# Second attention of a two-layer block model: the kernel gives the order of instructions on four engines

## The chip, the cores and the metric

The kernel runs on one core of a Trainium2 chip. The metric is the device time of one execution in microseconds, as the median of several runs. PE is the matrix engine, with PEld its weight loads; DVE, ACT and POOL are the vector, scalar and GpSimd engines; SP issues transfers.

## The reference

The input is 16 sequences of 256 tokens with 256 features in float32. Two layers follow each other, and every sub-layer is added to its input and normalized:

```
x = layernorm(x + L0_attn(x))   # receptance, key, value; a decaying scan over time
x = layernorm(x + L0_ffn(x))    # gated feed-forward, weights dequantized
x = layernorm(x + L1_attn(x))   # latent attention: 16 heads, two-sequence batches, causal softmax
x = layernorm(x + L1_ffn(x))    # 32 experts, 4 chosen per token, and a shared expert
```

The change is in the third line. There, for one sequence and one head:

```
cq     = rms_norm(x @ w_qa.T);  q = cq @ w_qb.T          # 128 plain and 64 rotated columns a head
ckv    = x @ w_kva.T;  k_pe = rotated(ckv[64:]);  c = rms_norm(ckv[:64])
scores = (q_nope . k_nope + q_pe . k_pe) * scale, masked above the diagonal
out    = softmax(scores) @ v;   x = layernorm(x + concat(out) @ w_o.T)
```

The fourth line needs a routing decision for each token (sigmoid scores, the best 3 of 8 groups, the best 4 experts in them) and a slot for each token and expert.

## The kernel before

The 4096 tokens are cut into 8 blocks of 512 tokens, which is two sequences each. The stages run one after the other: first attention, feed-forward, second attention, the rest of the shared expert, the experts, and the sum. The code is written for a tile framework whose scheduler decides the order of instructions on each engine from the dependencies and from its own costs; `tc.issue_after(x)` keeps a few instructions behind another one. Each engine then works through its own queue in that order.

In the second attention a step is a pair of heads of a block, so there are 64 steps. Keys and queries of a head are folded into the latent space beforehand (`w_q`, `w_qr`), and values with the output weights (`w_ov`).

- `latents(b)` (L742) is done once a block: eight PE transposes of the input, four latent products with squares on ACT, two inverse roots (`rsqrt`: DVE, then a power on POOL), scaling on DVE into `cq` and `kf`, rotation of the key part (`kr`), and twelve PE transposes, with copies by DVE (`cqT`) and ACT (`kT`).
- `queries` (L820) makes `q_ps` for both heads in two PSUM tiles of the tag `m`; `turn` (L837) rotates each with three DVE products from PSUM and one POOL addition.
- `attend` (L851) is one head in one sequence. PE writes scores in two parts, 128x128 and 128x256, which leave out the masked quarter. DVE adds the mask and takes the extreme (L868), ACT takes the exponential with its row sum (L878), DVE takes the reciprocals (L886, L887), POOL divides (L888).
- `keys_first` (L896) transposes the result on PE, ACT copies it. `contexts` (L906) multiplies it by the latents of the keys, two heads beside each other in the array.
- `stage_contexts` (L926) copies the contexts into `cT` on DVE (L935), and after four pairs multiplies by `w_ov`, which adds half an output to `x` (L945); after eight pairs `added` adds the other half and normalizes.
- `choose` (L554) and `place` (L636) route the block before: some sixty small DVE instructions and a few matmuls. `scatter` (L669) writes one token tile for one choice with an indirect transfer by POOL. `shared_glu` and `shared_down` (L688, L702) are the shared expert, done here for three blocks.

The PSUM has eight banks: three for the tag `m` (queries, latents, outputs, router and shared expert take turns in them), two for scores, two for transposes, one for contexts.

The loop over steps (L966) writes the queries of step i, the softmax of step i-1 and the contexts of step i-2, and the latents of the next block at its sixth step. The routing of a block is written into the first and third steps of the next block, its scatters into the softmax of steps 4 to 7. The scheduler moves all of this within the dependencies.

Of the kernel before, what the change touches and what calls it, by code (L numbers as in the profile page):

```python
# [86 lines left out]
def seq_postln_kernel(ctx: ExitStack, tc: tile.TileContext, a: dict, out: bass.AP, cap: int):  # L87
# [42 lines left out]
    def layernorm(ys, dsts):  # L130
        n = len(ys)
        mv = small.tile([P, n, 2], F32, tag=f"mv{n}", name="mv")
        for i, y in enumerate(ys):
            st = small.tile([P, 6], F32, tag="bn", name="bn")
            nc.vector.bn_stats(st, y)
            nc.vector.bn_aggr(mv[:, i, :], st)
        rstd = small.tile([P, n], F32, tag=f"rstd{n}", name="rstd")
        rsqrt(rstd, mv[:, :, 1], 1.0, LN_EPS)
        for i, (y, dst) in enumerate(zip(ys, dsts)):
            nc.vector.tensor_scalar(  # L140
                dst, y, mv[:, i, 0:1], rstd[:, i : i + 1], ALU.subtract, ALU.mult
            )

# [403 lines left out]

    SH_EARLY = 3
# [5 lines left out]
    def choose(b, psum, tag):  # L554

        xT = xTs[b] = transposed(b, mo_x, psum, tag)
        l_ps = psum.tile([P, BLK], F32, tag=tag, name="l_ps")[:, : GT * E].rearrange(
# [11 lines left out]

        last_of["PE"] = mm.ins  # L570

        sco = tl("sco", GT, E)
        nc.scalar.activation(sco, l_ps, AF.Sigmoid)
        sc = tl("sc", GT, E)
# [12 lines left out]
        tt_(gs.rearrange("p n g -> p (n g)"), m1, m2, ALU.add)  # L587

# [17 lines left out]
        )  # L606

# [3 lines left out]
        for k in range(K):  # L611
# [5 lines left out]
            if k < K - 1:  # L617
                nc.vector.scalar_tensor_tensor(
                    left, chosen[:, k], TAKEN, left, ALU.mult, ALU.add
                )  # L620
        big, wt = tl("big", K, GT, E), tl("wt", K, GT)
# [6 lines left out]
        tt_(wt, wt, top.unsqueeze(1).to_broadcast([P, K, GT]), ALU.mult)  # L628

# [4 lines left out]
        return sel, chosen, big, eq  # L634

    def place(b, psum, tag, chose):  # L636

        sel, chosen, big, eq = chose
# [87 lines left out]
    with ExitStack() as ph:  # L726
        pl = ph.enter_context(tc.tile_pool(name="lat", bufs=2))
        pq = ph.enter_context(tc.tile_pool(name="q2", bufs=3))
# [11 lines left out]
        X2 = X1 + HR  # L740

        def latents(b):  # L742


            xT = transposed(b, mo_x, ps_m, "m")
            lat = pl.tile([P, NTT, QLR + KVLR + DR], F32, tag="lat", name="lat", bufs=1)
            ss = pl.tile([P, 2, NTT], F32, tag="ss", name="ss")
            sq = pl.tile([P, QLR], F32, tag="sq", name="sq")
            for tt in range(NTT):
# [9 lines left out]
                nc.scalar.copy(lat[:, tt, :], ps)  # L759
                for k, (lo, n) in enumerate(((0, QLR), (QLR, KVLR))):  # L760
# [6 lines left out]
            rms = pl.tile([P, 2, NTT], F32, tag="rms", name="rms")  # L767
            rsqrt(rms[:, 0, :], ss[:, 0, :], 1.0 / QLR, RMS_EPS)
            rsqrt(rms[:, 1, :], ss[:, 1, :], 1.0 / KVLR, RMS_EPS)
            cq = pl.tile([P, NTT, 2 * P], F32, tag="cq", name="cq", bufs=1)  # L770
            kf = pl.tile([P, NTT, P], F32, tag="kf", name="kf")
            for tt in range(NTT):
# [9 lines left out]
                )  # L782
                nc.vector.scalar_tensor_tensor(
# [7 lines left out]
            kr = pl.tile([P, NTT, DR], F32, tag="kr", name="kr")  # L791
# [4 lines left out]

            cqT = pl.tile([P, 2, BLK], F32, tag="cqT", name="cqT")
            for j in range(2):
                ps = ps_m.tile([P, BLK], F32, tag="m", name="cqT_ps")
                for tt in range(NTT):  # L800
# [3 lines left out]
                nc.vector.tensor_scalar(  # L804
                    cqT[:, j, :], ps, q_ln[:, j : j + 1], None, ALU.mult
                )
            kT = pl.tile([P, BLK], F32, tag="kT", name="kT")
# [4 lines left out]
            return cqT, kf, kT  # L812
# [7 lines left out]
        def queries(cqT, pair):  # L820

            pss = []
            for k in range(2):
                ps = ps_m.tile([P, BLK], F32, tag="m", name="q_ps")
                mm = nc.tensor.matmul(  # L825
# [3 lines left out]
            with tc.issue_after(mm.ins):  # L829
                for k, ps in enumerate(pss):  # L830
                    rows = slice(k * QR, (k + 1) * QR)
                    nc.tensor.matmul(
                        ps, lhsT=w_qr[rows, pair, :], rhs=cqT[rows, 1, :], start=False, stop=True
                    )
            return [turn(ps, 2 * pair + k) for k, ps in enumerate(pss)]

        def turn(ps, h):  # L837
            qT = pq.tile([P, BLK], F32, tag="qT", name="qT", bufs=5)
# [10 lines left out]
        pool_last = [None]  # L849

        def attend(qT, kT, s):  # L851

            ps = ps_s.tile([P, 3 * P], F32, tag="s", name="s_ps")
            sm = pa.tile([P, 3 * P], F32, tag="sm", name="sm")
            pr = pa.tile([P, 3 * P], F32, tag="pr", name="pr", bufs=8)
            nm = pa.tile([P, 2], F32, tag="nm", name="nm")
            rs = pa.tile([P, 2], F32, tag="rs", name="rs")
            rr = pa.tile([P, 3], F32, tag="rr", name="rr")
            for i, (lo, hi) in enumerate(parts):
                nc.tensor.matmul(  # L860
                    ps[:, lo:hi],
                    lhsT=qT[:, s * S + i * P : s * S + (i + 1) * P],
                    rhs=kT[:, s * S : s * S + hi - lo],
                    start=True,
                    stop=True,
                )
            for i, (lo, hi) in enumerate(parts):
                nc.vector.tensor_tensor_reduce(  # L868
                    out=sm[:, lo:hi],
                    in0=ps[:, lo:hi],  # L870
                    in1=cst["mask"][:, lo:hi],
                    scale=-(DQ**-0.5),
                    scalar=-MASKED,
                    op0=ALU.add,
                    op1=ALU.min,
                    accum_out=nm[:, i : i + 1],
                )
                nc.scalar.activation(  # L878
                    pr[:, lo:hi],
                    sm[:, lo:hi],  # L880
                    AF.Exp,
                    bias=nm[:, i : i + 1],
                    scale=-1.0,
                    accum_out=rs[:, i : i + 1],
                )
            nc.vector.reciprocal(rr[:, :2], rs)  # L886
            nc.vector.reciprocal(rr[:, 2:], rs[:, 1:])  # L887
            pool_last[0] = nc.gpsimd.tensor_tensor(  # L888
                pr.rearrange("p (i k) -> p i k", k=P),
                pr.rearrange("p (i k) -> p i k", k=P),  # L890
                rr.unsqueeze(2).to_broadcast([P, 3, P]),
                ALU.mult,
            ).ins
            return pr

        def keys_first(pr):  # L896

            a_ps = ps_a.tile([P, 3 * P], F32, tag="a", name="a_ps")
            for i in range(3):
                nc.tensor.transpose(  # L900
                    a_ps[:, i * P : (i + 1) * P], pr[:, i * P : (i + 1) * P], ident
                )
            aT = pa.tile([P, 3 * P], F32, tag="aT", name="aT")
            return aT, nc.scalar.copy(aT, a_ps)  # L904

        def contexts(c_ps, prs, kf, s):  # L906


            aTs, copies = zip(*[keys_first(pr) for pr in prs])
            for i in range(2):  # L910
                for k, aT in enumerate(aTs):
                    mm = nc.tensor.matmul(
                        c_ps[k * KVLR : (k + 1) * KVLR, i * P :],
# [5 lines left out]
                    if i == k == 0:  # L919
                        after(mm.ins, copies[1].ins, "beside the other head's")  # L920
            last_of["ctx"] = mm.ins

        NP = NH // 2
        blocks = {}

        def stage_contexts(b, p, prs):  # L926
            kf = blocks[b][1]
            half_p = p % (NP // 2)
            if half_p == 0:
                cTs[0] = pc.tile([P, NP // 2, BLK], F32, tag="cT", name="cT")  # L930
            cT = cTs[0]
            c_ps = ps_c.tile([P, 2, S], F32, tag="c", name="c_ps")
            for s in range(2):
                contexts(c_ps[:, s, :], prs[2 * s : 2 * s + 2], kf, s)
            nc.vector.tensor_copy(cT[:, half_p, :], c_ps.rearrange("p s t -> p (s t)"))  # L935
            if half_p == NP // 2 - 1:
                os = []
                for s in range(2):
                    ps = ps_m.tile([P, BLK], F32, tag="m", name="o_ps").rearrange(
                        "p (k d) -> p k d", k=2  # L940
                    )
                    for k in range(2):
                        at = (2 * s + k) * P
                        for j in range(NP // 2):
                            nc.tensor.matmul(  # L945
                                ps[:, k, :],
                                lhsT=cT[:, j, at : at + P],
                                rhs=w_ov[:, p - half_p + j, :],
                                start=(j == 0),
                                stop=(j == NP // 2 - 1),  # L950
                            )
                        os.append(ps[:, k, :])
                    if p < NP - 1:
                        x2 = xs[b][:, 2 * s : 2 * s + 2, :D]
                        nc.vector.tensor_tensor(x2, ps, x2, ALU.add)
                if p == NP - 1:
# [3 lines left out]
        def begin(b):  # L960
            blocks[b] = latents(b)
# [272 lines left out]
```

## Time and profile before

| | |
|---|---|
| time, median of 3 runs (lowest to highest) | 2430.03 us (2429.53 to 2431.76) |
| the profiled execution, and its span from first to last instruction | 2428.3 us, 2426.5 us |
| mean granted PE clock | 0.964 |
| PE, DVE, ACT, POOL busy, share of the span | 91%, 55%, 29%, 34% |
| second attention: first transposes of its first block to its last output matmul | 1213.5 to 2170.1 us |
| eight context products of block 5, first start to that of block 6 | 1834.4 to 1951.3 us |

A row of the timeline reads: start, time until the last one ends, engine, line, operation, output <- inputs, shapes and how often in a row. A float32 matmul of the code stands as two records, a transpose as one; matmuls overlap, so the distance between starts says what one costs, and the duration is longer. A row of groups reads: line, engine, operation, shapes and count, then busy time and mean nanoseconds of one, then the idle time of the engine just before and what ended it. In rows of stretches, each engine's busy time has its number of instructions behind it, and the last three columns are the granted PE clock, the share of the transfer engines and GB/s.

### The profile page before, as it was taken

What the parts mean: (1) busy time and instruction counts of PE and PEld (TensorE: products, weight loads), DVE (VectorE), ACT (ScalarE), POOL (GpSimd) and SP (SyncE); (2) the same over time, 40 slices, a digit from 0 to 9 for tenths busy, and PEclk for the clock granted to TensorE, in tenths of its full rate; (3) what the DMA queues carried; (4) which work ended last, traced back from release to release, by engine and by line L of the source; (5) the groups of instructions that cost most, each with busy time, mean ns of one, the idle gap of its engine ahead of it and who ended that gap; (6) DMA issues with size and microseconds to landing.
All of it is one profiled execution on the core that took longest, in us unless ns stands there. A gap on an engine that the chain in (4) does not pass through costs nothing. (4 is left out here: it accounts for less than half of the span.)

```text
span 2426.5 us, 27654 instructions
## 1 busy us (share of the span) xinstructions
PE 2203.7 (91%) x8832; PEld 1325.7 (55%) x8832; DVE 1332.7 (55%) x4052; ACT 708.9 (29%) x2013; POOL 826.9 (34%) x932
## 2 busy tenths in 40 slices
PE   8499999999999999999989888999898888888937
PEld 4255555555555555455556555555555555555826
DVE  4163545454454433222376868686878887855513
ACT  3021212222121112111145445353535344331202
POOL 3021212122211210000054464645555647452671
PEclk9699999999999999999999999999999999999968
DMA  9620000000000003000000000000000000042746
GB/s 301 196 59 0 9 1 9 1 9 1 0 1 1 0 1 111 0 1 0 1 1 1 5 30 2 14 2 13 1 3 2 3 2 3 1 148 86 147 64 263
DMA packets 75793, 90.53 MB, mean 37 GB/s; under 512 B 13719, under 2 KB 66011, under 8 KB 75520
## 3 DMA queue, kind: packets, MB, share of 16 engines
q1 hardware_dynamic: 46208, 59.46, 7.3%
q10 hardware_dynamic: 17152, 21.44, 2.9%
q0 software_dynamic: 12288, 7.87, 2.3%
q8 instruction: 70, 1.15, 0.2%
q14 instruction: 75, 0.61, 0.1%
HBM read 58.29 MB, written 45.21 MB: 43 GB/s over the span
## 5 line engine op out<-in xcount | busy, mean ns | idle before, releaser
L342 POOL TENSOR_TENSOR wkv<-su,r_sb 128x512 f32<-128x512 f32 x128 | 165.3, 1292 | 719.8 <-DVE su L333 685.8
L319 DVE TENSOR_TENSOR kv<-k_sb,proj 128x512 f32<-128x512 f32 x128 | 88.0, 687 | 450.6 <-PE proj L298 406.5
L878 ACT ACTIVATE pr<-sm,nm 128x128 f32<-128x128 f32 (+1 forms) x512 | 228.0, 447 | 251.5 <-DVE nm L868 249.8
L298 PE MATMUL proj<-xm,w_Wr 128*128 128x512 f32 x512 | 242.7, 597 | 35.4 <-ACT k_sb L315 35.4
L888 POOL TENSOR_TENSOR pr<-pr,rr 128x384 f32<-128x384 f32 x256 | 210.6, 829 | 125.5 <-DVE rr L887 76.6
L298 PE MATMUL proj<-xm,w_Wk 128*128 128x512 f32 x512 | 242.5, 596 | 6.8 <-DVE xm L284 6.8
L347 PE MATMUL o_ps<-w_o,wkv 128*128 128x256 f32 x1024 | 245.2, 379 | 0.3 <-POOL st L322 0.2
L347 PEld LDWEIGHTS o_ps<-w_o,wkv 128*128 128x128 f32 x1024 | 194.4, 190 | 89.6 <-issue 67.8
L844 POOL TENSOR_TENSOR qT<-qT,turned 128x512 f32<-128x512 f32 x128 | 166.7, 1306 | 222.1 <-DVE turned L843 214.9
L298 PE MATMUL proj<-xm,w_Wv 128*128 128x512 f32 x512 | 241.4, 594 | 0.0
L315 ACT COPY k_sb<-proj 128x512 f32<-128x512 f32 x128 | 74.9, 585 | 559.5 <-PE proj L298 505.3
L860 PE MATMUL s_ps<-kT,qT 128*128 128x128 f32 (+1 forms) x1024 | 220.9, 352 | 8.7 <-DVE nm L868 6.2
L860 PEld LDWEIGHTS s_ps<-kT,qT 128*128 128x128 f32 x1024 | 152.5, 203 | 61.6 <-DVE nm L868 23.5
L298 PEld LDWEIGHTS proj<-xm,w_Wr 128*128 128x128 f32 x512 | 97.9, 192 | 156.0 <-issue 118.2
L868 DVE CUSTOM_DVE_ANT_0 sm<-s_ps,const 128x128 f32<-128x128 f32 (+1 forms) x512 | 159.6, 352 | 37.5 <-PE s_ps L860 32.3
L324 DVE TENSOR_TENSOR_SCAN st<-decay,kv 128x255 f32<-128x255 f32 x256 | 162.6, 677 | 3.8
L674 POOL DMA_INDIRECT xp_d<-xs,dest x128 | 128.5, 1004 | 100.8 <-DVE dest L659 74.2
L298 PEld LDWEIGHTS proj<-xm,w_Wv 128*128 128x128 f32 x512 | 97.7, 191 | 117.3 <-issue 116.5
L900 PE MATMUL a_ps<-const,pr 128*128 128x128 f32 x768 | 131.3, 286 | 32.4 <-POOL pr L888 30.1
L904 ACT COPY aT<-a_ps 128x384 f32<-128x384 f32 x256 | 117.4, 471 | 142.8 <-PE a_ps L900 139.2
L128 POOL TENSOR_TENSOR rstd<-rs_t,nhalf 128x4 f32<-128x4 f32 x32 | 32.5, 1017 | 350.8 <-DVE rs_t L127 345.9
L825 PE MATMUL q_ps<-cqT,w_q 128*128 128x512 f32 x256 | 135.8, 631 | 8.5 <-DVE turned L843 8.5
(166 smaller groups left out, 3363.0 us busy)
## 6 DMA issues: line engine op xcount, KB each, us to landing
w_e<-in_W_experts_dram SPq DMA_DIRECT2D x32, 384.0 KB
sum<-zeros ACTq DMA_DIRECT2D x2, 4224.0 KB
part<-sum SPq DMA_DIRECT2D x16, 512.0 KB
xp_d<-empty ACTq DMA_DIRECT2D x1, 5300.0 KB
xe<-xp_d SPq DMA_DIRECT2D x32, 165.6 KB
xb<-in_xT_dram SPq DMA_DIRECT2D x16, 256.0 KB
xs<-in_x_dram SPq DMA_DIRECT2D x32, 128.0 KB
sum<-acc SPq DMA_DIRECT2D x16, 256.0 KB
```

What stands on the lines that cost most here:

```text
L298: nc.tensor.matmul(ps, lhsT=w3[name][:, c, h * P : (h + 1) * P], rhs=xm[:, c, :], start=(c == 0), stop=(c == DC - 1),)
L324: nc.vector.tensor_tensor_scan(st[:, s, 1:], decay[:, h : h + 1].to_broadcast([P, S - 1]), kv[:, s, : S - 1], 0.0, ALU.mult, ALU.add,)
L342: nc.gpsimd.tensor_tensor(wkv, su, r_sb, ALU.mult)
L347: nc.tensor.matmul(os[tt], lhsT=wkv[:, tt * P : (tt + 1) * P], rhs=w_o[:, h, :], start=(h == 0), stop=(h == NH - 1),)
L674: put = nc.gpsimd.indirect_dma_start(out=xp_d[:, :], out_offset=bass.IndirectOffsetOnAxis(ap=dest[:, k, t : t + 1], axis=0), in_=xs[b][:, ...
L825: mm = nc.tensor.matmul(ps, lhsT=w_q[:, 2 * pair + k, :], rhs=cqT[:, 0, :], start=True, stop=False)
L844: nc.gpsimd.tensor_tensor(qT, qT, qr, ALU.add)
L860: nc.tensor.matmul(ps[:, lo:hi], lhsT=qT[:, s * S + i * P : s * S + (i + 1) * P], rhs=kT[:, s * S : s * S + hi - lo], start=True, stop=True,)
L868: nc.vector.tensor_tensor_reduce(out=sm[:, lo:hi], in0=ps[:, lo:hi], in1=cst["mask"][:, lo:hi], scale=-(DQ**-0.5), scalar=-MASKED, op0=ALU ...
L878: nc.scalar.activation(pr[:, lo:hi], sm[:, lo:hi], AF.Exp, bias=nm[:, i : i + 1], scale=-1.0, accum_out=rs[:, i : i + 1],)
L888: pool_last[0] = nc.gpsimd.tensor_tensor(pr.rearrange("p (i k) -> p i k", k=P), pr.rearrange("p (i k) -> p i k", k=P), rr.unsqueeze(2).to_ ...
L900: nc.tensor.transpose(a_ps[:, i * P : (i + 1) * P], pr[:, i * P : (i + 1) * P], ident)
```

## The change

The whole second attention now stands under `tc.manual_schedule` for PE, DVE, ACT and POOL: on these engines its instructions run in the order in which the code writes them. Step n of the new loop writes the scores and softmax of pair n+1, the queries of pair n+2 and the contexts of pair n-1, interleaved by hand. `latents` and `choose` with `place` (now `route`) are generators, of eight and nine parts. Their parts, the halves of the output (`output`, now by sequence), the two halves of the norm (`moments`, `normalize`) and the parts of the shared expert are put at two places in each step, by the pair's number p in its block.

Some work changes its form. A softmax now covers both sequences of a head: one reciprocal of 128x4 takes the place of four, and POOL divides in one instruction of 128x2x128 and one of 128x2x256 in place of two of 128x384. The copies of `cT` and the scalings of `cqT` go from DVE to ACT. The buffers of `qT` become six, `pr` becomes six tiles of two sequences, and `sq`, `kr` have one or are taken anew. The scatters of a block come two blocks later, two or three in each step but the first, so those of block 6 now follow the attention.

The diff, cut; `parts`, `scores` and `exps` of the new class `Softmax` hold what `attend` held:

```
-    def choose(b, psum, tag):
+    def route(b, psum, tag):
...
         xT = xTs[b] = transposed(b, mo_x, psum, tag)
+        yield
...
-                nc.vector.tensor_scalar(
-                    cqT[:, j, :], ps, q_ln[:, j : j + 1], None, ALU.mult
-                )
+                nc.scalar.activation(cqT[:, j, :], ps, AF.Copy, scale=q_ln[:, j : j + 1])
...
+            def divide(self):
+                rr = pa.tile([P, 2, 2], F32, tag="rr", name="rr")
+                nc.vector.reciprocal(rr, self.rs)
+                for i, (lo, hi) in enumerate(parts):
+                    nc.gpsimd.tensor_tensor(
+                        self.pr[:, :, lo:hi],
+                        self.pr[:, :, lo:hi],
+                        rr[:, :, i : i + 1].to_broadcast([P, 2, hi - lo]),
+                        ALU.mult,
+                    )
...
-            nc.vector.reciprocal(rr[:, :2], rs)
-            nc.vector.reciprocal(rr[:, 2:], rs[:, 1:])
-            pool_last[0] = nc.gpsimd.tensor_tensor(
-                pr.rearrange("p (i k) -> p i k", k=P),
-                pr.rearrange("p (i k) -> p i k", k=P),
-                rr.unsqueeze(2).to_broadcast([P, 3, P]),
-                ALU.mult,
-            ).ins
...
-            nc.vector.tensor_copy(cT[:, half_p, :], c_ps.rearrange("p s t -> p (s t)"))
...
+        def output(b, half, s):
+            cT = cTs[b, half]
+            ps = ps_m.tile([P, BLK], F32, tag="m", name="o_ps").rearrange("p (k d) -> p k d", k=2)
+            for k in range(2):
+                at = (2 * s + k) * P
+                for j in range(NP // 2):
+                    nc.tensor.matmul(
+                        ps[:, k, :],
+                        lhsT=cT[:, j, at : at + P],
+                        rhs=w_ov[:, half * NP // 2 + j, :],
+                        start=(j == 0),
+                        stop=(j == NP // 2 - 1),
+                    )
+            x2 = xs[b][:, 2 * s : 2 * s + 2, :D]
+            nc.vector.tensor_tensor(x2, ps, x2, ALU.add)
...
+        def first_place(b, p):
+            last = b - 1
+            if p == 3 and last >= 0:
+                x = x_t[last * NTT : (last + 1) * NTT]
+                normalize(x, x, *norms.pop(last))
+            if p == 4:
+                step_latents(b + 1)
+            if p >= 5:
+                step_route(last)
+        def second_place(b, p):
+            last = b - 1
+            if p == 0:
+                step_route(last - 1)
+            if p <= 5 or p == 7:
+                step_latents(b + 2 if p == 7 else b + 1)
+            if p in (1, 2) and last >= 0:
+                output(last, 1, p - 1)
+                if p == 2:
+                    norms[last] = moments(x_t[last * NTT : (last + 1) * NTT])
+            if 3 <= p:
+                step_route(last)
+            if p in (5, 6):
+                output(b, 0, p - 5)
+            if p == 7:
+                shared(last, 0)
+            if p == 0:
+                shared(last - 1, 1)
+            if p == 4:
+                shared(last - 1, 2)
+                shared(last - 1, 3)
+        def scatters(b, p):
+            if b >= 0 and p:
+                lo = 3 * (p - 1) if p < 3 else 6 + 2 * (p - 3)
+                return [(b, j) for j in range(lo, lo + (3 if p < 3 else 2))]
+            return []
+        NS = NB * NP
+        engines = {nc.tensor.engine, nc.vector.engine, nc.scalar.engine, nc.gpsimd.engine}
+        with tc.manual_schedule(engines=engines):
+            qTs, sms = {}, {}
+            for _ in range(8):
+                step_latents(0)
+            step_latents(1)
+            for n in range(-2, NS + 1):
+                b, p = divmod(n, NP)
+                todo = scatters(b - 2, p)
+                def one_scatter():
+                    if todo:
+                        scatter(todo[0][0], [todo.pop(0)[1]])
+                scored = n + 1 if 0 <= n + 1 < NS else None
+                asked = n + 2 if 0 <= n + 2 < NS else None
+                seen = n - 1 if 0 <= n - 1 < NS else None
+                if scored is not None:
+                    kT = latent[scored // NP][2]
+                    heads = sms[scored] = []
+                    qT2 = qTs.pop(scored)
+                    heads.append(Softmax())
+                    for s in range(2):
+                        heads[0].scores(qT2[0], kT, s)
+                        heads[0].exps(s)
+                if asked is not None:
+                    q_ps = queries(latent[asked // NP][0], asked % NP)
+                    qTs[asked] = []
+                if n >= 0:
+                    first_place(b, p)
+                if scored is not None:
+                    heads[0].divide()
+                if seen is not None:
+                    pair = sms.pop(seen)
+                    kf = latent[seen // NP][1]
+                    part, j = divmod(seen % NP, NP // 2)
+                    if j == 0:
+                        cT = cTs[seen // NP, part] = pc.tile(
+                            [P, NP // 2, BLK], F32, tag="cT", name="cT"
+                        )
+                    c_ps = ps_c.tile([P, 2, S], F32, tag="c", name="c_ps")
+                    aTs0 = keys_first(pair, 0)
+                if asked is not None:
+                    qTs[asked].append(turn(q_ps[0], 2 * asked))
+                one_scatter()
+                if scored is not None:
+                    heads.append(Softmax())
+                    heads[1].scores(qT2[1], kT, 0)
+                    heads[1].exps(0)
+                    heads[1].scores(qT2[1], kT, 1)
+                if seen is not None:
+                    contexts(c_ps, *aTs0, kf, 0)
+                    aTs1 = keys_first(pair, 1)
+                if scored is not None:
+                    heads[1].exps(1)
+                if asked is not None:
+                    qTs[asked].append(turn(q_ps[1], 2 * asked + 1))
+                one_scatter()
+                if scored is not None:
+                    heads[1].divide()
+                if n >= 0:
+                    second_place(b, p)
+                if seen is not None:
+                    contexts(c_ps, *aTs1, kf, 1)
+                    nc.scalar.copy(cT[:, j, :], c_ps.rearrange("p s t -> p (s t)"))
+                one_scatter()
+            last = NB - 1
             for s in range(2):
...
+                output(last, 1, s)
+            x = x_t[last * NTT :]
+            layernorm(x, x)
...
-        chose = behind_last(choose, NB - 1, ps_t, "t")
+        scatter(NB - 2, range(GT * K))
+        routing = route(NB - 1, ps_t, "t")
+        for _ in range(ROUTE_PARTS - 1):
+            behind_last(next, routing)
...
```

## The prediction

> **What bounds the kernel now.** I read the page first, for where the engines are busy.
>
> ```profile
> PE 2203.7 (91%) x8832; PEld 1325.7 (55%) x8832; DVE 1332.7 (55%) x4052; ACT 708.9 (29%) x2013; POOL 826.9 (34%) x932
> ...
> PE   8499999999999999999989888999898888888937
> ...
> DVE  4163545454454433222376868686878887855513
> ```
>
> The second attention is slices 20 to 35. In it PE falls from 9 to 8 and DVE rises from 3 to 8. Both are high and neither is full, so the question is whether they are full at the same moments. The chain that ended last covers only the final microseconds, so I went on to busy time in stretches, cut at the starts of the context products (c_ps) of the eight pairs of one block, block 5:
>
> ```profile
> core 0: us, PE busy (x) PEld busy (x) DVE busy (x) ACT busy (x) POOL busy (x), PEclk, DMA share, GB/s
> 1834.40:1847.20 12.80, 12.25 (x76) 7.40 (x75) 9.30 (x29) 6.30 (x14) 4.40 (x4) 1.00 0.00 1
> 1847.20:1860.80 13.60, 9.12 (x53) 5.09 (x51) 12.24 (x36) 4.00 (x11) 5.25 (x5) 1.00 0.00 0
> 1860.80:1872.50 11.70, 10.70 (x59) 8.10 (x59) 10.25 (x59) 8.79 (x34) 6.44 (x8) 0.71 0.01 3
> 1872.50:1878.30 5.80, 3.40 (x31) 2.32 (x32) 5.66 (x21) 3.34 (x12) 2.91 (x4) 1.00 0.00 0
> 1878.30:1907.00 28.70, 26.98 (x134) 18.53 (x135) 22.48 (x75) 9.99 (x40) 16.12 (x16) 1.00 0.02 4
> 1907.00:1913.90 6.90, 4.74 (x35) 3.05 (x37) 6.25 (x26) 4.97 (x22) 6.14 (x7) 1.00 0.02 5
> 1913.90:1940.00 26.10, 23.10 (x108) 13.04 (x108) 21.87 (x70) 7.56 (x28) 15.44 (x16) 1.00 0.01 2
> 1940.00:1951.30 11.30, 10.87 (x69) 8.39 (x66) 6.87 (x42) 7.11 (x30) 9.81 (x12) 1.00 0.02 4
> ```
>
> Pairs take 6 to 29 us. In 1847 to 1861 DVE is full (routing of the block before, with turns) and PE has a third idle; in 1940 to 1951 it is the other way round. The block takes 116.9 us, with PE busy 101.2 and DVE 94.9. The limits take turns. PE's busy time also holds the tails of pipelined matmuls, so I priced PE by the distance between starts, in PE's timeline:
>
> ```profile
> 1881.83 1.88 PE L825 MATMUL q_ps<-cqT,w_q 128*128 128x512 f32 x4
> 1883.64 1.13 PE L832 MATMUL q_ps<-cqT,w_qr 64*128 64x512 f32 x4
> 1884.70 7.17 PE L945 MATMUL o_ps<-w_ov,cT 128*128 128x256 f32 x32
> ```
>
> Queries cost 1.81 + 1.06 = 2.87 us a pair; 32 output records run from 1884.70 to 1891.71, 0.22 each. The same reading gives 0.66 for the scores of a head in one sequence, 0.33 for its three transposes and 0.80 for the contexts of a sequence.
>
> **PE by place.** I call the eight steps of a block p=0 to 7. A step is 4x0.66 + 2.87 + 4x0.33 + 2x0.80 = 8.4 us of PE. The change adds at p=0 one latent product (1.1) and the placing (0.5); p=1 and 2 a latent product and half an output (16 x 0.22 = 3.5); p=3 a latent product and eight transposes (0.9); p=4 the router (1.8); p=5 twelve transposes (1.4) and 3.5; p=6 3.5; p=7 0.9. Per place: 10.0, 13.0, 13.0, 10.4, 10.2, 13.3, 11.9, 9.3, in sum 91. Shared experts add 3.4 at p=7, then 3.4 at p=0 and 3.5 at p=4 of the next block, for three blocks. No PE work is added or removed.
>
> **DVE by place.** These groups are of block 5 alone:
>
> ```profile
> L841 DVE TENSOR_TENSOR qT<-q_ps,const 128x512 f32<-128x512 f32 x16 | 11.0, 689 | 4.5 <-PE q_ps L832 4.2
> L935 DVE COPY cT<-c_ps 128x512 f32<-128x512 f32 x8 | 5.4, 681 | 0.1
> L886 DVE RECIPROCAL rr<-rs 128x2 f32<-128x2 f32 x32 | 5.1, 161 | 6.3 <-ACT pr L878 4.1 <-POOL pr L888 1.1 <-ACT aT L904 0.5
> L887 DVE RECIPROCAL rr<-rs 128x1 f32<-128x1 f32 x32 | 4.6, 143 | 0.0
> ```
>
> Removed from DVE in a block: the cT copies (5.4, now ACT), 64 reciprocals (9.7) against 16 on 128x4 (0.16 each, 2.6), two cqT scalings (0.74 each, now ACT): 14.0 less, so 81 of the 94.9. A step keeps four masks (0.22 + 0.34), two turns (2.14) and two reciprocals: 6.8. The spread work, by its own rows, is 3.3, 0.7, 2.7, 1.5, 5.1, 4.7, 7.5, 3.2 at p=0 to 7, so DVE has 10.1, 7.5, 9.5, 8.3, 11.9, 11.5, 14.3, 10.0, in sum 83 with starting gaps.
>
> The larger of PE and DVE at each place sums to 96.0 us. ACT gains about 6 us on 52, and POOL stays near 66.5: its 32 divisions of 128x384 (828 ns) become 32 of 128x2x128 and 128x2x256. The trace has no such shape; at equal time per element they cost the same 26.5, at the rate of the 128x512 addition (1331 ns) 32. I take the first, as it is the same operation with the same broadcast. Both lie inside POOL's free half.
>
> **Waits that the fixed order adds.** I followed one block through the written order. On PE the second scores of a step wait for the first head's masks, done 3 us earlier; the last contexts wait for ACT's copies, which queue behind an exponential that waits for a DVE mask behind a turn. Around that loop a step needs about 8.6 us, less than any place has. What is exposed comes from the three buffers of ps_m, two of which hold queries until the turns end: at p=3 the second xT_ps waits 0.7, at p=5 kT_ps waits 2.7 with outputs, contexts and next scores queued behind it, at p=7 contexts wait 1.7 for DVE's arrears from p=6. At p=4 DVE waits about 1 for two powers on POOL. Part of this is absorbed where the other engine is the limit: 98 us a block, plus 11 with shared experts. Block 0 (no routing) comes to 85, blocks 1 to 7 to 102, 109, 109, 105, 98, 98, 91: 797 us.
>
> One thing is missing from this. DVE instructions that read and write only SBUF stretch when POOL computes beside them:
>
> ```profile
> L534 DVE TENSOR_TENSOR chosen<-const,codes x32: 266/292/875, 1370.9 to 2201.3; 128x128 f32<-128x128 f32 x32
> L793 DVE TENSOR_TENSOR kr<-lat,const x8: 280/1362/1572, 1220.6 to 2023.8; 128x128 f32<-128x128 f32 x8
> ```
>
> Minimum and maximum differ by up to 1.3 us, the length of a POOL addition, while the turns from PSUM hold 689. Routing now lies beside POOL's work at every place. Bounds: nothing (the rows used are already means with half of them hit) to 46 such instructions times half a 0.83 us division, 19 us a block. I take 1.5, as only p=4 to 7 are DVE's and the means hold most of it: 10 us in all. The Trainium skill, "SBUF — State Buffer", section "SBUF: two separate sides", calls this an exclusive lock between GpSimd and a VectorE instruction with two SBUF inputs or in a two-port mode, held for a whole instruction. The trace agrees (1362 against 280 ns); by that rule alone the upper end would hold, and it is my third rival.
>
> The clock was 0.71 in one stretch above and 0.96 over most blocks; I add 1 us a block for dips that stay. The Trainium skill, "TensorE: Matmul & The Clock Gate", section "Why this matters for your kernels", ties a drop to an idle gap over about 3 us; my longest PE wait is 2.7, so by it these 8 us would not occur.
>
> **Ends.** The first latents start at 1213.5 and the last output ends at 2170.1: 956.6 us. After: 28.5 to the first full step, 797 + 10 + 8 = 815, and 17 for the last contexts, the placing, two outputs and the norm: 860.5, so 96 less. After it, 16 scatters of block 6 stand on POOL before the power of the last norm in the built order; 16 x 1.28 = 20.5 us from the placing on, of which 12 lie beside a shared expert on PE, and routing block 7 starts some 5 later. The rest of the tail, and everything before 1213 in the built order, is as it was. Net 91: 2428.3 (the profiled execution: span 2426.5 and 1.8 around it) becomes 2337; the median of the runs, 2430.0, lies 1.7 higher, so 2339.
>
> **Rivals.** (1) Slower: lock-step through ps_m. If all side work of PE starts only after the second turn (9.8 us into a step) and DVE's second share only after that, a step is 9.8 + 3.0 + 0.8 + 2.3 = 15.9, and 64 of them with 45.5 and the 5 of the tail make 1068, 111 more: 2541. It turns slower above 14.2 a step. For it: one tag of three, and queues that can't pass each other. Against: only one tile at p=3, 5 and 7 needs the held buffer. 0.10. (2) Evener work leaves no dips, and waits hide in arrears: the larger engine at each place only, 35 us better: 2304. 0.12. (3) The lock: 7 to 10 us more in each of seven blocks, about 2395 to 2410 with some waits behind it. For it the kr row; against, that POOL computes less than half the time. 0.10. That the order is not kept is out: the built instructions follow the written steps.
>
> **How the numbers follow.** Forecast (2310 to 2375) 0.66, lock-step 0.10, evener 0.12, lock 0.10, no change 0.02. A measurement tells 0.2% (5 us) from none. Faster is 0.66 + 0.12 + 0.10 = 0.88, same 0.02, slower 0.10. From 2285 to 2400 leaves out lock-step, no change, half of the lock case and a little below: 0.2.
>
> **What would show it.** Right: in the changed profile the pairs of a block lie between 10 and 16 us with the longest at p=5 and 6, a plain block near 100, DVE near 81 busy in it, POOL's divisions 0.55 and 1.1 us, clock at 0.97 or more, and PE waiting for the turn before kT_ps. Wrong: steps all near 16, PE's waits on turned or c_ps above 3 us a step, eq and chosen near 0.8 us, or POOL above 12 us a step.

## The result, and the profile after

| | before | after |
|---|---|---|
| time, median of 4 runs (lowest to highest) | 2429.8 us (2429.5 to 2431.8) | 2374.0 us (2372.2 to 2380.8) |
| profiled execution, span | 2428.3, 2426.5 us | 2374.0, 2371.8 us |
| mean granted PE clock | 0.964 | 0.969 |
| second attention, first transposes to end of the last output matmul | 956.6 us | 885.2 us (1216.0 to 2101.2) |
| a plain block (block 5, without shared experts) | 116.9 us | 106.1 us |
| from there to the end of the span | 256.4 us | 270.6 us |

The ratio is 0.9774 (0.9754 to 0.9794): 56 us faster, where 91 were forecast. The attention gave 71 of 96, the tail after it lost 14 instead of 5, and the attention began 2.5 later. The page's first row:

```profile
PE 2166.5 (91%) x8832; PEld 1319.2 (56%) x8832; DVE 1292.8 (55%) x3572; ACT 760.2 (32%) x2099; POOL 822.8 (35%) x932
```

Shares hardly move, since span and work shrink together; DVE's busy time fell by 40 us, not by 8 times 14. The stretches of block 5, cut again at the starts of the context products. Each of them runs from the middle of a step to the middle of the next; the first starts in the step p=1, and I call them by the p in which they start:

```profile
core 0: us, PE busy (x) PEld busy (x) DVE busy (x) ACT busy (x) POOL busy (x), PEclk, DMA share, GB/s
1809.20:1822.50 13.30, 13.30 (x72) 9.21 (x72) 8.88 (x27) 7.02 (x26) 9.93 (x11) 1.00 0.01 2
1822.50:1835.80 13.30, 13.30 (x73) 9.22 (x72) 10.26 (x39) 7.04 (x26) 9.51 (x10) 1.00 0.01 3
1835.80:1847.50 11.70, 11.00 (x65) 7.10 (x64) 8.76 (x34) 7.89 (x28) 9.36 (x11) 1.00 0.02 3
1847.50:1861.20 13.70, 10.90 (x69) 7.39 (x68) 12.42 (x40) 8.48 (x24) 7.67 (x8) 1.00 0.01 1
1861.20:1877.20 16.00, 13.74 (x80) 9.75 (x80) 15.14 (x45) 7.58 (x25) 7.92 (x9) 1.00 0.01 2
1877.20:1891.80 14.60, 12.62 (x69) 8.49 (x68) 13.97 (x39) 5.77 (x21) 7.69 (x8) 1.00 0.01 2
1891.80:1903.80 12.00, 9.89 (x60) 6.39 (x60) 10.56 (x34) 6.80 (x24) 9.37 (x10) 1.00 0.02 4
1903.80:1915.30 11.50, 10.75 (x63) 6.69 (x62) 9.86 (x36) 6.96 (x26) 4.56 (x5) 1.00 0.00 0
sum 106.10, PE 95.50 PEld 64.23 DVE 89.84 ACT 57.55 POOL 66.00; mean PE 11.94 PEld 8.03 DVE 11.23 ACT 7.19 POOL 8.25
```

Pairs now take 11.5 to 16 us in place of 6 to 29. At p=1 and 2 PE is busy throughout. At p=4, 5 and 6 DVE is over 90% busy and PE has 2.0 to 2.8 us idle: the missing time is there. The changed forms, and PE's waits for a turn, over the attention:

```profile
L912 DVE RECIPROCAL rr<-rs 128x4 f32<-128x4 f32 x16 | 2.8, 175 | 4.4 <-ACT pr L901 4.2
```

```profile
L914 POOL TENSOR_TENSOR pr<-pr,rr 128x512 f32<-128x512 f32 x128 | 133.2, 1040 | 0.0
...
L914 POOL TENSOR_TENSOR pr<-pr,rr 128x256 f32<-128x256 f32 x128 | 80.4, 628 | 214.7 <-DVE rr L912 173.4 <-PE a_ps L927 22.0 <-PE s_ps L879 17.3
```

```profile
PE c_ps L940 <- ACT aT L931: 24.9, 26, 3.1
...
PE kT_ps L827 <- DVE turned L860: 15.2, 7, 2.2
...
PE xT_ps L157 <- DVE turned L860: 6.9, 11, 0.7
```

The first two fences are from the groups (of block 5, then of POOL over the whole program), the third from the waits between 1240 and 2101 us: total, times, longest. POOL's two divisions take 0.63 and 1.04 us. Contexts wait for ACT's copies by 0.4 us a step on average (24.9 over 64). kT_ps waits 2.2 us once a block, as the walk through the written order had it.

### The profile page after: what moved, and what is told of

It is laid out like the page before. It is cut to its first block, busy times and chain, and to the rows that moved or that the text cites. A ratio compares the mean times of both kernels' runs of the same rounds, so it can differ in the third digit from the quotient of the medians.

```text
span 2371.8 us, 26672 instructions
## 1 busy us (share of the span) xinstructions
PE 2166.5 (91%) x8832; PEld 1319.2 (56%) x8832; DVE 1292.8 (55%) x3572; ACT 760.2 (32%) x2099; POOL 822.8 (35%) x932
## 5 line engine op out<-in xcount | busy, mean ns | idle before, releaser
L914 POOL TENSOR_TENSOR pr<-pr,rr 128x256 f32<-128x256 f32 (+1 forms) x256 | 208.0, 834 | 214.7 <-DVE rr L912 173.4
L879 PE MATMUL s_ps<-kT,qT 128*128 128x128 f32 (+1 forms) x1024 | 196.6, 335 | 18.8 <-DVE nm L890 12.1
L890 DVE CUSTOM_DVE_ANT_0 sm<-s_ps,const 128x128 f32<-128x128 f32 (+1 forms) x512 | 154.8, 354 | 29.2 <-PE s_ps L879 26.6
L879 PEld LDWEIGHTS s_ps<-kT,qT 128*128 128x128 f32 x1024 | 144.2, 191 | 41.8 <-issue 24.7
L197 DVE TENSOR_TENSOR hT<-sg,u_ps 128x512 f32<-128x512 f32 x64 | 43.9, 685 | 179.1 <-PE u_ps L187 179.1
L305 PEld LDWEIGHTS proj<-xm,w_Wk 128*128 128x128 f32 x512 | 97.7, 191 | 77.4 <-issue 63.7
L940 PE MATMUL c_ps<-aT,kf 128*64 128x256 f32 (+1 forms) x1024 | 111.5, 339 | 25.0 <-ACT aT L931 24.9
```

Of the source, the lines that this page charges most:

```text
L305: nc.tensor.matmul(ps, lhsT=w3[name][:, c, h * P : (h + 1) * P], rhs=xm[:, c, :], start=(c == 0), stop=(c == DC - 1),)
L879: nc.tensor.matmul(ps[:, lo:hi], lhsT=qT[:, s * S + i * P : s * S + (i + 1) * P], rhs=kT[:, s * S : s * S + hi - lo], start=True, stop=True,)
L890: nc.vector.tensor_tensor_reduce(out=sm[:, lo:hi], in0=self.ps[s][:, lo:hi], in1=cst["mask"][:, lo:hi], scale=-(DQ**-0.5), scalar=-MASKED, ...
L914: nc.gpsimd.tensor_tensor(self.pr[:, :, lo:hi], self.pr[:, :, lo:hi], rr[:, :, i : i + 1].to_broadcast([P, 2, hi - lo]), ALU.mult,)
L940: mm = nc.tensor.matmul(c_ps[k * KVLR : (k + 1) * KVLR, s, i * P :], lhsT=kf[:, 2 * s + i, :KVLR], rhs=aT[:, : 2 * P] if i == 0 else aT[:, ...
```

## The experiments

### Is it the order, or the lighter forms?

forms_only is the kernel before with the new forms and the scheduler's order; order_only is the changed kernel with the copies of cT and the scalings of cqT back on DVE and four reciprocals a softmax; POOL's two divisions stay in their new form.

```
# forms_only, in the kernel before
-            nc.vector.tensor_copy(cT[:, half_p, :], ...)     +  nc.scalar.copy(cT[:, half_p, :], ...)
-                nc.vector.tensor_scalar(cqT[:, j, :], ...)   +  nc.scalar.activation(cqT[:, j, :], ps, AF.Copy, ...)
-        def attend(qT, kT, s):                               +  def attend(qT, kT):   # both sequences, one rr, two divisions
# order_only, in the changed kernel: the first two lines the other way round, and
-                nc.vector.reciprocal(rr, self.rs)
+                for s in range(2):
+                    for i in range(2):
+                        nc.vector.reciprocal(rr[:, s, i : i + 1], self.rs[:, s, i : i + 1])
```

> The kernel before, with the scheduler's order, and only the new forms: cT copies and cqT scalings on ACT, one softmax for both sequences of a head with one reciprocal and two POOL divisions. Theory (the order makes the gain): DVE loses 9.7 us of work a block, but PE and DVE still take turns as the limit, so less than half of the 56 us comes: 2405 to 2430. Rival (the lighter DVE makes the gain): 2370 to 2390.

Measured: 2440.3 us (ratio to before 1.0040, 1.0025 to 1.0054). The forms by themselves make the kernel 10 us slower: with the scheduler's order plain blocks still take 116 to 119 us, with pairs of 4 to 32. The scheduler made another order for them (block 5 begins with pairs of 5.6 and 28.3 us, where before had 12.8 and 13.6), so this run changes more than the forms.

> The changed kernel with its order, but cT copies and cqT scalings back on DVE and four reciprocals per softmax instead of one. Theory (order): each step gets 0.62 + 0.42 us of DVE work back, which shows only where DVE is the limit (p=4, 5, 6) and at p=5 the 1.4 of cqT: about 4.5 us a block, some 35 us in all, 2400 to 2415. Rival (forms): the whole gain is lost, 2425 to 2435.

Measured: 2402.4 us (0.9871, 0.9853 to 0.9889). The new order with the old copies, scalings and reciprocals brings 28 us, and with it the lighter forms bring another 28. So half of the gain needs both: under the new order the forms are worth 28 us, and under the scheduler's they brought nothing. That forms_only would be slower, I had not expected.

### Is it that the routing is spread?

route_lumped keeps the order, and puts the seven middle parts of the routing at one place.

```
-            if p >= 5:
-                step_route(last)          # first half of a step
...
-            if 3 <= p:
-                step_route(last)          # second half
+            if p == 3:
+                step_route(last)
+            if p == 6:
+                for _ in range(7):
+                    step_route(last)
```

> The changed kernel with the seven middle parts of the routing (router to weights) all at p=6; the rest is as it was. Theory (the gain is that the parts are spread): DVE gets some 15 us at once while PE waits, p=6 goes from 14.6 to about 26 and p=4, 5, 7 give back 6 to 8; 2400 to 2420. Rival (it is enough that the order of the steps is fixed): within 10 us of 2374.

Measured: 2431.1 us (0.9996, 0.9985 to 1.0006), all of the gain gone. Its p=6 in block 5, and the block (columns as above):

```profile
1911.70:1938.50 26.80, 15.84 (x85) 11.18 (x84) 21.72 (x72) 8.62 (x24) 6.21 (x6) 0.79 0.00 1
...
sum 119.10, PE 101.11 PEld 68.16 DVE 87.71 ACT 57.87 POOL 65.55; mean PE 12.64 PEld 8.52 DVE 10.96 ACT 7.23 POOL 8.19
```

DVE has 21.7 us of work in that stretch and PE 11 us with nothing to do, after which the clock is granted at 0.79. DVE's work in the block is smaller than in the changed kernel (87.7), and still the block is 13 us longer. The place was expected (26), and the price of it too low by at least 11. So with the routing in one lump at p=6 the fixed order gains nothing; a lump at another place was not tried.

### What is the stretch beside POOL worth?

no_division leaves out POOL's divisions; the softmax stays undivided.

```
-                for i, (lo, hi) in enumerate(parts):
+                for i, (lo, hi) in enumerate(parts[:0]):
                     nc.gpsimd.tensor_tensor(self.pr[:, :, lo:hi], ...)
```

> The changed kernel without POOL's divisions, so the softmax stays undivided: POOL loses 26 us a block. Theory (DVE is the limit at p=4 to 6, lengthened by POOL's instructions beside it): kr, kf, eq, rank and left fall back by over half of their 9.3 us excess in a block, p=4 to 6 become shorter by 4 to 5 us together, 30 to 40 us in all: about 2335 to 2345. Rival (the excess is not on the path, or comes from something else): under 10 us, 2364 to 2374, with the same long kr and eq.

Measured: 2344.0 us (0.9633, 0.9616 to 0.9650), 30 less. Two lines of DVE in the changed kernel, then the same in no_division (count: least, median, longest ns):

```profile
L610 DVE TENSOR_SCALAR rank<-rank x8: 180/1016/1019, 1411.3 to 2129.3; 128x32 f32<-128x32 f32 x8
...
L813 DVE TENSOR_TENSOR kr<-lat,const x8: 278/1692/1693, 1227.4 to 1960.8; 128x128 f32<-128x128 f32 x8
```

```profile
L610 DVE TENSOR_SCALAR rank<-rank x8: 180/181/182, 1406.2 to 2101.9; 128x32 f32<-128x32 f32 x8
...
L813 DVE TENSOR_TENSOR kr<-lat,const x8: 276/281/288, 1226.8 to 1933.0; 128x128 f32<-128x128 f32 x8
```

For each DVE instruction of block 5 I took the time above the least duration of the same instruction, and summed those of 0.1 us and more: 6.0 us before, 9.3 after, 4.0 here and 6.4 in route_lumped. What stays here lies beside POOL's additions. p=4 to 6 and the block in no_division:

```profile
1827.60:1838.10 10.50, 10.50 (x69) 7.36 (x68) 10.23 (x40) 8.71 (x24) 4.63 (x4) 1.00 0.01 1
1838.10:1853.30 15.20, 13.77 (x81) 9.75 (x80) 13.22 (x44) 7.54 (x24) 4.73 (x4) 1.00 0.01 3
1853.30:1866.40 13.10, 12.57 (x69) 8.49 (x68) 12.51 (x39) 5.74 (x21) 4.51 (x4) 1.00 0.01 1
...
sum 99.50, PE 94.68 PEld 64.15 DVE 84.49 ACT 57.85 POOL 39.68; mean PE 11.83 PEld 8.02 DVE 10.56 ACT 7.23 POOL 4.96
```

The block takes 99.5 in place of 106.1, and DVE is 5.3 us less busy, which is the 9.3 less 4.0. A shorter way through the softmax is no rival for it: in the changed kernel's attention PE's weight loads waited for a division by 1.1 us in all, and no other engine waited for one. Of the 6.6 us, 5.5 are at p=4 to 6 and 1.1 at p=0, where the placing of the block before lies.

### Can DVE's work be moved to where it has room?

latents_early moves `kf`, `kr` and `cq` to p=1 and 2, with the latent products a step or two earlier; both_early moves the routing a place earlier as well.

```
-            if p <= 5 or p == 7:
-                step_latents(b + 2 if p == 7 else b + 1)
+            for _ in range((2, 1, 1, 0, 1, 0, 1, 2)[p]):
+                step_latents(b + 2 if p > 5 else b + 1)
# both_early, besides: a yield after each of the four choices, and in the first half of a step
+            for _ in range((0, 0, 0, 0, 1, 1, 2, 1)[p]):
+                step_route(last)
```

> The changed kernel; the parts of the next block's latents come earlier: xT at p=6, products at p=7 and 0 (two each), kf and kr at p=1, cq at p=2, the transposes to cqT and kT at p=4. Theory (DVE is the limit at p=4 to 6 and has room at p=1 and 2): p=4 falls from 13.7 to about 11.6, p=1 and 2 from 13.3 to 12 to 12.5, p=5 by 1.4: some 4 us a block, 2340 to 2350. Rival (what is late is a chain through both engines, wherever the work lies): less than 8 us, 2366 to 2374.

> As latents_early, and the routing in eleven parts one place earlier: router at p=4, the four choices one by one at p=5 and 6, weights at p=7, the placing at p=0 as before; the shared down products at p=3. Theory: PE and DVE come to 9 to 13 us at every place, with PE slightly the larger; a plain block takes 96 to 99 us in place of 106, so 2305 to 2325. Rival (POOL's instructions lengthen DVE's wherever they are, and a step cannot fall under some 13 us): 2335 or more.

Measured: 2382.6 us (0.9792, 0.9773 to 0.9812) and 2389.8 us (0.9825, 0.9805 to 0.9844): by the medians 9 and 16 us slower than the changed kernel. Its own ratio is 0.9774 (0.9754 to 0.9794), so for latents_early the loss is not clear of the noise; that the forecast gains did not come is. My expectations failed. In block 5 of latents_early p=5 does fall, from 16.0 to 12.3, but p=6 rises from 14.6 to 20.7. Three stretches of it:

```profile
1877.00:1884.00 7.00, 7.00 (x40) 4.23 (x39) 6.56 (x23) 2.71 (x11) 1.69 (x2) 1.00 0.01 3
1884.00:1890.00 6.00, 1.58 (x13) 1.10 (x11) 5.83 (x18) 2.84 (x11) 3.89 (x4) 0.89 0.00 1
1890.00:1898.00 8.00, 7.96 (x29) 6.10 (x30) 6.31 (x13) 1.31 (x3) 3.87 (x4) 0.66 0.01 0
```

In the middle one DVE is full and PE nearly idle. The transposes of xT, which now stand at p=6, need two buffers of ps_m, and the output a third, while DVE is behind with the routing and its turns still hold the queries: xT_ps waited 1.9 for `turned`, o_ps 2.6. The clock fell to half for 6.8 us behind that. This is the first rival of the prediction, lock-step through ps_m, at one place: a place is cheap for PE only if DVE is not in arrears there.

kf_first and kf_and_route_first try it without new ps_m tiles in the second half of a busy step. They build on loads_spread (below) and are compared with it.

```
# kf_first: kf and kr at the first half of p=4; cq at its second half, on ACT
-                nc.vector.tensor_scalar(cq[:, tt, :P], lat[:, tt, :P], rms[:, 0, tt : tt + 1], None, ALU.mult)
+                nc.scalar.activation(cq[:, tt, :P], lat[:, tt, :P], AF.Copy, scale=rms[:, 0, tt : tt + 1])
# kf_and_route_first, besides
-            if p >= 5:                    +            if p >= 4:                # first half
-            if 3 <= p:                    +            if p in (3, 4, 5, 7):     # second half
```

> As loads_spread (2361); kf and kr move within p=4 from the end of the step, where POOL adds and divides beside them, to its first half, and the eight cq scalings go from DVE to ACT at the end of p=4. Theory (p=4 is DVE's place, with 1.7 of cq and 3.1 of stretch on kf and kr): p=4 falls from 13.7 to 10.5 to 11.5, and the arrears of p=5 with it; 2 to 4 us a block, 2335 to 2348. Rival (work ahead of the turns holds the buffers of ps_m, and PE's tiles wait, as in latents_early): 2356 or more.

> As kf_first, and the routing half a step earlier from the router on: router in the first half of p=4, group sums at its end, ranks in the first half of p=5, two choices at its end, two in the first half of p=6, weights and rest as before. Theory (DVE's load by place becomes 12.1, 13.6, 11 against PE's 10.2, 13.3, 11.9 at p=4, 5, 6): p=5 from 16.0 to about 14, p=6 from 14.6 to about 12.5, a block near 100 in place of 106: 2315 to 2330. Rival (at p=5 turns become later by the ranks and five tiles of ps_m wait for them): p=5 stays at 16 or more, 2340 to 2365.

Measured: 2371.1 us (0.9749, 0.9733 to 0.9765) and 2359.5 us (0.9712, 0.9692 to 0.9732), against 2360.8 for loads_spread. The first missed its forecast by 23 us. Its stretch excess in block 5 fell to 6.8 us as meant, but p=4 stayed at 13.9 there, where 10.5 to 11.5 were forecast. Its attention took 885.0 us, which is no gain: four profiles with the attention as in the changed kernel lie between 882.0 and 891.0 (the changed kernel, tail_power_first, loads_spread and tail_shifted). Its tail was 13 us longer than that of loads_spread. In the second the attention took 872.8 us: p=6 came down to 12.3 and in plain blocks p=7 to 10.4, while p=5 stayed at 17 to 20, as the rival had it, by which the turns come later and five tiles of ps_m wait for them. Its tail, too, was 14 us longer, so little of the gain in the attention was left.

### The tail

In the changed kernel, the 16 scatters of block 6 end on POOL just before the power of the last norm, and PE waits:

```profile
2116.56 0.97 POOL L685 DMA_INDIRECT xp_d<-xs,dest  x1 [0.30 <-issue]
2117.55 1.05 POOL L128 TENSOR_TENSOR rstd<-rs_t,nhalf 128x4 f32<-128x4 f32 x1
...
2119.20 1.94 PE L157 MATMUL xT_ps<-const,xs 128*128 128x128 f32 x8 [4.95 <-DVE xs L144]
```

These 4.95 us are the 5 of the prediction. From 2117.2 the clock is at half for 13.7 us. Up to the first matmul of the experts the tail takes 81.7 us, 71.6 before. tail_power_first puts the scatters behind the power; loads_spread also spreads the 25 loads of expert weights.

```
+        with tc.issue_after(last_power):
+            scatter(NB - 2, range(GT * K))
# loads_spread, besides: two loads at once, then three after each shared_up and shared_rest
+                experts.append(load_expert(len(experts), last_of["PE"]))   # waits for that matmul
```

> The changed kernel; the 16 scatters of block 6 are held behind the power of the last norm on POOL. Theory: the 5 us wait of xT_ps before routing block 7 goes, and with it the 13.7 us at half clock that follow PE's idle 4.95 us, so 9 to 11 us less than the changed kernel: about 2364. Rival (the clock falls there anyway, or the scatters delay the experts instead): 5 us less or nothing, 2369 to 2374.

Measured: 2373.9 us (0.9759, 0.9743 to 0.9776), no gain; the rival's figure. The 5 us wait is gone, but another stop has come in its place:

```profile
2121.20 1.28 ACT L584 ACT_TABLE_LOAD   x1
...
2123.13 1.95 PE L159 MATMUL xT_ps<-const,xs 128*128 128x128 f32 x8
...
2127.06 0.97 POOL L687 DMA_INDIRECT xp_d<-xs,dest  x1 [0.30 <-issue]
2130.54 0.28 ACT L584 ACTIVATE sco<-l_ps 128x128 f32<-128x128 f32 x1 [8.05 <-remote]
```

ACT's sigmoid waits for one semaphore, that of PE's l_ps, whose records end before those of xT_ps at 2125.1, and starts at 2130.5. The clock is again at half for 13.7 us, and the stretch to the experts takes 84.6.

> As tail_power_first, and the 25 loads of expert weights, which follow the attention in one lot at some 390 GB/s (27 us), are held behind PE's work for the shared experts, three at a time. Theory: in that lot the engines' own instruction pages come late; with it gone ACT's idle 6.7 and 8.0 us without a releaser and the half clock after them go, so 10 to 15 us less than tail_power_first: 2360 to 2364. Rival (the wait has another cause): within 4 us of 2374.

Measured: 2360.8 us (0.9704, 0.9687 to 0.9721), as forecast: the stop and the half clock are gone, and the stretch takes 69.9. But kf_first has the same tail, with the loads spread, and stops for 9.5 us at that very instruction. So the loads are not the whole cause, and that the time was met does not show the theory. Two more runs tested whether an instruction packet comes late, by 40 small ACT copies in earlier steps:

```
+                if 0 <= n < 40:
+                    nc.scalar.copy(spare, ident[:, :1])
```

> As tail_power_first (2374), with 40 copies of one column more on ACT, one at the end of each of the first 40 steps, where ACT has room (0.2 us each, off the path). Theory (ACT's stop of 8.0 us before the sigmoid of block 7 is an instruction packet that comes late, with an 8 KB packet in the middle of it, and its place goes with the number of ACT's instructions before it): the stop goes elsewhere or vanishes, 2361 to 2368. Rival (the stop belongs to the table load or to the scatters beside it): it stays before the sigmoid, 2372 to 2378.

> As kf_and_route_first (2359.5), with the same 40 copies on ACT. Theory (late instruction packet): the 8.8 us stop before the sigmoid goes and with it the 17 us of half clock: 2346 to 2352. Rival (table load or scatters): 2358 to 2362.

Measured: 2372.4 us (0.9747, 0.9729 to 0.9766) and 2360.0 us (0.9691, 0.9671 to 0.9711). The stops stayed where they were, with the same 8.0 and 8.8 us. The theory of the packet falls. What the five kernels with the stop share is that the sigmoid starts 2.5 us after the last scatter of block 6 ends; in loads_spread it starts 8.5 us before that, with the scatters running. What lets it go there stays open.

## Why the prediction was right, though its time was 35 us too low

**The mechanism.** It was right. route_lumped undoes the spreading alone, and all of the gain goes; order_only puts DVE's heavier forms back, and half goes. So the gain needs even places and a lighter DVE. In block 5 the steps lie between 11.4 and 16.0, the longest at p=5 and 6, as written down. The clock rose only to 0.969 (0.97 was asked for).

**PE by place** holds. At p=1 and 2 the sums were 13.0, and 13.3 was measured; the waits named at kT_ps (2.7) and xT_ps (0.7) came out at 2.2 and at most 0.7.

**DVE by place** was too low: 81 forecast, 89.8 measured. 4.3 of the 8.8 is a sum wrongly made. I took 9.7 us of reciprocals out at their full durations, but these overlap, and in the trace they cover 5.8 us of DVE's time, the new ones 2.5; cT covers 5.0, not 5.4. So the change takes 9.7 us from a block and not 14.0. 3.3 more is stretch (6.0 to 9.3 us), and 1.2 are not accounted for.

**The stretch beside POOL** was priced too low. I took 1.5 us a block above the rows of before, with the reason that their means held most of it. They held 6.0 us; 3.3 more came. The spreading brings it: with the routing in a lump the excess is 6.0 us before and 6.4 in route_lumped, spread out it is 9.3. Of the 41 routing and latent instructions of a block that are lengthened at least once in either profile (blocks 1 to 6), 9.5 were so before, by 0.53 us on average, and 13 after, by 0.70. Why a lump is spared was not looked into. no_division prices the divisions' whole part, old and new, at 6.6 us of a plain block for 5.3 us of DVE.

**What each of the two cost.** A plain block took 106.1 us where the prediction's 98, 1.5 and 1 made 100.5. I estimate the shares, as no run separates them. At the price in no_division, 3.3 us of stretch cost 4.1, which is 2.6 above my 1.5. In order_only block 5 takes 3.5 us longer with DVE 7.3 us busier; at that price the 4.3 us of the wrong sum cost 2.1. Together that is 4.7 of the 5.6 us.

**The third rival.** The truth is between my forecast and the lock, which had 7 to 10 us more a block; its time (2395 to 2410) was not reached, nor its upper bound of 19 us a block: the whole excess is 9.3. The Trainium skill, "SBUF — State Buffer", section "SBUF: two separate sides", says that the shared port is held for the whole instruction by whichever starts first. The trace agrees: 1016 against 180 ns for `rank` is 0.84 more, less than the 1.04 of a division.

**The sum over the attention.** The six blocks with routing took 5.5 us more each than forecast, 33 in all (blocks 1 to 4: 457 for 435, which is 425 and 2.5 each; 5 and 6: 212 for 201). The first block, the last one and both ends together came out some 8 shorter. That gives 885 for 860.5.

**The clock.** I added 8 us for dips that stay. From the first contexts to the last there were five dips of 3.4 us at half clock, so 8.5 us lost. Four of them start within 1.5 us of kT_ps in blocks 1 to 4. The one of block 1:

```profile
1405.20:1407.40 2.20, 0.38 (x3) 0.39 (x4) 2.14 (x6) 2.20 (x8) 0.30 (x1) 0.97 0.00 0
1407.40:1410.80 3.40, 3.40 (x11) 2.76 (x10) 3.33 (x4) 1.08 (x2) 3.14 (x3) 0.52 0.00 0
```

PE had been idle for 2.17 us before kT_ps, and then the clock is 0.52. The rule of the Trainium skill that the prediction weighed ("TensorE: Matmul & The Clock Gate", section "Why this matters for your kernels": a drop behind a gap of over about 3 us) would have had none of these, as PE's gaps before the five dips are 2.16 to 2.59 us. The trace differs, and the measurement decides for the 8 us. But no length of gap alone decides here: three more waits of 2.2 us before kT_ps, and one of 3.12 us before c_ps in block 6, had no dip behind them. Transposes stand on both sides of the gap at kT_ps; whether the clock counts them like other matmuls, no run tested.

**The tail.** The wait of 5 us was right in place and size. That the clock would then be at half for 13.7 us was left out. From the last output to the first expert matmul the tail took 10.1 us more than before, and from there to the end 4.0 more, whose cause stays open. The attention began 2.5 us later, where I had put nothing; 1.7 of it can be the 3.4 us at half clock at 1205.9, which before does not have.

**The rivals.** Lock-step through ps_m did not come as a whole (14.2 us a step was the turning point; a plain block has 13.3 on average), but latents_early shows it at one place, for 6 us. Evener work than forecast did not come.

## What to carry to other kernels

Sum what a change takes off an engine by the time in which nothing else runs on it, not by the durations in the groups, which overlap. Before spreading small SBUF work over steps, ask what POOL does at each of the new places: a mean that was measured in lumps does not price it. Work for PE that needs a shared PSUM buffer is cheap only in places where the engine that frees the buffers is not behind.

Of the kernels that leave nothing out, kf_and_route_first (2359.5, and 2360.0 with the 40 copies) and loads_spread (2360.8) took the least time, each about 0.6% below the changed kernel.

## What the runs showed of the hardware that I had not expected

Beside POOL not only instructions with two SBUF inputs are stretched: `rank`, a TENSOR_SCALAR with one input of 128x32, goes from 180 to 1016 ns. TENSOR_REDUCE is not: the one that makes `rank` just before takes 420 or 421 ns all eight times, in five of which a division of POOL runs throughout. Behind four of seven waits of PE of 2.2 us came 3.4 us at half clock, and none behind the other three. And ACT stood for 8.0 to 9.5 us at an instruction whose only wait was for PE, after PE's records had ended, until 2.5 us after the last of 16 scatters; with the loads of expert weights moved, one of the kernels was free of it, and three others were not.
